# Two fused cross-attention layers on one core: the first layer's row maxima, turned kind by head and brought in by two transfers of four heads

## The chip, the cores and the metric

The kernel runs on one core of one Trainium2 chip. The metric is the device time of one execution in microseconds (us). Three executions before the change took 1526.58, 1529.79 and 1536.33 us, with a median of 1529.79 us. One more execution was recorded by the hardware profiler, and all profile lines come from it.

Engines are named as the profile names them. PE is TensorE (matmuls; PEld are its weight loads), DVE is VectorE, ACT is ScalarE, POOL is GpSimd, and SP is SyncE, which here only issues transfers. Rows marked ACTq or SPq are transfers (DMAs) issued by ACT or SP.

## The reference

Two attention layers follow each other on `x` (16 batches, 256 positions, 320 channels, 20 heads of 16). Both read the same context of 256 tokens. What matters here is the first layer, which splits the context in 77 text tokens and 179 image tokens and takes a softmax over each of the two kinds apart:

```python
q, k_text, v_text = hidden_states @ Wq, text @ Wk, text @ Wv
probs = softmax(einsum('bhqd,bhkd->bhqk', q_h, k_h) * scale)
text_out = einsum('bhqk,bhkd->bhqd', probs, v_h)
scores = einsum('bhqd,bhkd->bhqk', q_h, ip_k_h) * scale
text_probs = softmax(einsum('bqc,bkc->bqk', q, k_text) * scale)
q_sem = einsum('bqk,bkc->bqc', text_probs, text)
sem = einsum('bqc,bnc->bqn', q_sem, ip) * scale
ip_probs = softmax(scores + 0.5 * sem[:, None]) * spatial_mask[None, None, :, None]
ip_out = einsum('bhqk,bhkd->bhqd', ip_probs, ip_v_h)
out = (text_out + ip_out) @ Wout + bout + residual
```

So each query row of each head needs two maxima in this layer: one over its 77 text scores and one over its 179 image scores. The second layer is of the same family, with 252 text tokens, 4 image tokens and one maximum for a row.

## The kernel before

The code counts the layers from 0, so the first layer of the reference has names that end in 0, and its 80 units of work are k = 0 to 79. A unit is four heads of one batch (five units a batch). The second layer has another 80 units, k = 80 to 159, and names that end in 1. One loop runs over all units (`slot0`, then `slot1`), and next to each unit the steps of other tasks (keys, queries, the semantic map, the output projection, weights) are called at times that tables in the code give.

**A unit of the first layer.** Its operands lie in two stacks, `qs` and `ks`, of 128 partitions by four heads by 256. There are four buffers of each, used in turn. Partitions 0 to 47 hold the 16 numbers of a head in three parts (rounded part and remainder), 48 to 124 hold the text map (`tph` on the side of `qs`, `M` on the side of `ks`), and partitions 125 and 126 (`XROW + T0` and the next) hold in `ks` two rows of minus ones, one for text tokens and one for image tokens, and in `qs` the two row maxima of each head. So a product over all 127 rows gives scores from which the maxima are already taken away. The steps are:

1. `stacks0(k)`, four units ahead: SP loads `ks` and `qs` (the DMAs from `kd`, `qd`, `tph`, `M`).
2. `score0(k, t)` for each half t of the queries: four matmuls (line 738) fill the only score tile `S` of this layer, and two DVE reductions (lines 739 and 740) write the maxima over text and over image tokens to `mn`.
3. `maxima0(k)`: two small matmuls by the identity (line 746) turn `mn` into 8 rows of 256 in a bank X of PSUM, ACT copies them to the SBUF tile `mt` (line 748), and four transfers issued by ACT (line 750) bring two rows each, a head's text and image maximum, to partitions 125 and 126 of that head in `qs`. For units 0 and 1 SP issues them. `mt` has one buffer, so the next copy waits for these transfers.
4. `turned0(k, t)`, a slot later: four matmuls (line 762) into two T tiles, two exponentials on ACT (line 765) to `P`, two products on POOL (line 768).
5. `attend0(k)`: 24 matmuls (line 795), then DVE and POOL work (`settle0`).

In slot k the code gives PE this order: maxima of unit k+1, scores of unit k+2 (t = 0), turned scores of unit k (t = 0), other tasks, attend of unit k-1, scores of unit k+2 (t = 1), turned scores of unit k (t = 1), loads of unit k+4, other tasks. The second exponentials of unit k are tied behind the last maxima transfer of unit k+1 (`queued(exp, issues[k + 1])`).

**Other tasks that the prediction names.** `semantic0` adds two score parts: ACT copies one from its bank X (`sp`, line 663), DVE adds the other (line 664) and so frees the bank, then come a maximum (667), the exponential (ACT, 672) and the division (ACT, 676). `context` casts loaded tokens (`rawc`) on ACT to `cta` and `ctb` (line 160). `split` casts the attended rows `hT` on ACT to `ho` (lines 592 and 593) for the output projection (lines 605 and 608). `evacuate` takes keys and queries out of a bank X (lines 160, 267 to 270). There are three X banks, used in turn by all tasks.

**What sets the order.** PE's order is that in which the code calls. In the loop over units the orders of DVE, ACT, POOL and SP are made by the framework's scheduler when the program is built, with its own estimates of durations; `queued` and `anchor` tie a few instructions. In the built program the transfers of SP and ACT share eight semaphores, which they take in turn. A transfer may be issued only when the transfer that had its semaphore before, eight earlier in the program, has landed; where another wait implies this, the wait is left out. A waiting transfer holds everything behind it on its engine.

Of the kernel before, what the change touches and what calls it, by code (L numbers as in the profile page):

```python
# [9 lines left out]
FR = mybir.dt.float32r  # L10
AF = mybir.ActivationFunctionType
ALU = mybir.AluOpType
AX = mybir.AxisListType
# [10 lines left out]
T0 = 77  # L24
# [7 lines left out]
KS0 = 127  # L32
KS1 = 50
XROW = 48
# [15 lines left out]
def xattn2(  # L50
# [27 lines left out]
    nc = tc.nc  # L78
    f = lambda ap: ap.bitcast(F32)
    mm = nc.tensor.matmul  # L80
# [9 lines left out]
    def bank(tag="X"):  # L90
        return ps.tile([128, 512], F32, tag=tag, name=tag, bufs=BANKS[tag])
# [10 lines left out]
    def scores(kept=False):  # L102

        s = whole if kept else ps.tile([128, 1024], F32, tag="S", name="S", bufs=1)
        return s.rearrange("p (h t) -> p h t", h=4)
# [4 lines left out]
    def buf(tag, shape, dtype=F32, bufs=1, name=None):  # L110
        if tag in ("wB", "wD", "vr", "raw"):
            return sb.tile(shape, dtype, tag=tag, name=name or tag, bufs=bufs)
        size = 1
        for d in shape[1:]:
            size *= d
        if tag not in slots:
            slots[tag] = [0, dtype] + [const_tile([128, max(size, words.get(tag, 0))], f"{tag}_{i}", dtype) for i in range(bufs)]
        n, kind, *ring = slots[tag]
        assert kind == dtype and len(ring) == bufs, tag
        slots[tag][0] += 1  # L120
        t = ring[n % bufs][: shape[0], :size]
        names = "abcd"[: len(shape) - 1]
        if len(names) > 1:
            t = t.rearrange(f"p ({' '.join(names)}) -> p {' '.join(names)}", **dict(zip(names, shape[1:])))
        return t

    def const_tile(shape, tag, dtype=F32):
        return const.tile(shape, dtype, tag=tag, name=tag)
# [7 lines left out]
    ident_r = const_tile([128, 128], "ident_r", FR)  # L136
# [15 lines left out]
    def anchor(inst):  # L152
        anchors[inst.ins.engine] = inst
        return inst
# [574 lines left out]
    maxes, issues = {}, {}  # L729

    def score0(k, t):
        Q, K = QK[k]
        if t == 0:
            maxes[k] = buf("mn", [128, 2, 4, 2], FR, bufs=2)
        mn = maxes[k]
        sp = scores(True)
        for h in range(4):
            mm(sp[:, h], Q[: XROW + T0, h, t * 128 : (t + 1) * 128], K[: XROW + T0, h], start=True, stop=True)  # L738
        nc.vector.tensor_reduce(mn[:, t, :, 0], sp[:, :, :T0], axis=AX.X, op=ALU.max)  # L739
        anchor(nc.vector.tensor_reduce(mn[:, t, :, 1], sp[:, :, T0:], axis=AX.X, op=ALU.max))  # L740

    def maxima0(k, queue=nc.scalar):
        Q, mn = QK[k][0], maxes[k]
        mp = bank()
        for t in range(2):
            mm(mp[:8, t * 128 : (t + 1) * 128], mn[:, t].rearrange("p h a -> p (h a)"), ident_r, start=True, stop=True)
        mt = buf("mt", [8, S], FR)
        nc.scalar.copy(mt, mp[:8, :S])  # L748
        for h in range(4):
            issues[k] = queue.dma_start(f(Q[XROW + T0 : KS0, h]), f(mt[2 * h : 2 * h + 2]))  # L750

    def turned0(k, t):

# [386 lines left out]
    for c in range(B // 2):  # L1140
        n, k = 10 * c, [("k0", c)] if c else []
# [34 lines left out]
    def ahead(k, t):  # L1176
        if k < NS:
            score0(k, t)
        else:
            both1(k - 2, t)  # L1180
# [5 lines left out]
    def begin():  # L1186
# [15 lines left out]
        stacks0(2)  # L1202
        parts(k0)
        score0(0, 0)
        parts(v1)
        score0(0, 1)
        get("m0t", 1)
        maxima0(0, nc.sync)
        parts(v1)
        get(*v1)  # L1210
# [3 lines left out]
        score0(1, 1)  # L1214
        parts(*[("s0", 1)] * 3)
        maxima0(1, nc.sync)
        parts(("s0", 1), ("s0", 1), ("k0", 1))
        resid0.append(load(xT_d[0], "xc"))
# [97 lines left out]
```

## Time and profile before

| what | value |
|---|---|
| median of three runs | 1529.79 us |
| profiled execution, whole time | 1526.5 us |
| its span, first to last instruction | 1524.7 us |
| PE busy in the span | 1436.7 us (94%) |
| POOL busy | 1209.5 us (79%) |
| DVE busy | 1114.5 us (73%) |
| ACT busy, its DMA issues not counted | 891.4 us (58%) |

In the profiled execution the first units' work starts at about 50 us, the first layer's loop runs from about 70 to 706 us, and the second layer to the end. A group's row names line, engine, operation and tiles. A row of waits says which instruction waited for which, then the total, the number of times and the longest (us). In a timeline the brackets at a row's end give the idle time of the engine before it and what ended it. The clock column (PEclk) is the granted TensorE clock as a share of full speed.

### The profile page before, as it was taken

What the parts mean: (1) busy time and instruction counts of PE and PEld (TensorE: products, weight loads), DVE (VectorE), ACT (ScalarE), POOL (GpSimd) and SP (SyncE); (2) the same over time, 40 slices, a digit from 0 to 9 for tenths busy, and PEclk for the clock granted to TensorE, in tenths of its full rate; (3) what the DMA queues carried; (4) which work ended last, traced back from release to release, by engine and by line L of the source; (5) the groups of instructions that cost most, each with busy time, mean ns of one, the idle gap of its engine ahead of it and who ended that gap; (6) DMA issues with size and microseconds to landing.
All of it is one profiled execution on the core that took longest, in us unless ns stands there. A gap on an engine that the chain in (4) does not pass through costs nothing.

```text
span 1524.7 us, 36323 instructions
## 1 busy us (share of the span) xinstructions
PE 1436.7 (94%) x12726; PEld 1159.4 (76%) x12726; DVE 1114.5 (73%) x2543; ACT 891.4 (58%) x2037; POOL 1209.5 (79%) x1529
## 2 busy tenths in 40 slices
PE   6789999999999989879999999999999999999996
PEld 6678888888888868667777777777777777777764
DVE  5466767676767677876787877787777777787784
ACT  5346565656565645546666666666666666666561
POOL 4269898989888976789678787878787787878695
PEclk9899999999999999999999999999999999999998
DMA  6766766676767675776354344444444444533411
GB/s 210 206 189 180 214 190 212 187 219 188 218 185 221 187 205 138 215 200 180 98 146 127 106 129 129 120 121 135 112 116 135 119 118 121 144 106 105 111 33 37
DMA packets 228818, 233.07 MB, mean 153 GB/s; under 512 B 38410, under 2 KB 198508, under 8 KB 228620
## 3 DMA queue, kind: packets, MB, share of 16 engines
q1 hardware_dynamic: 226428, 229.44, 52.6%
q8 instruction: 102, 1.67, 0.5%
q10 hardware_dynamic: 2208, 1.30, 0.3%
q14 instruction: 80, 0.66, 0.1%
HBM read 118.04 MB, written 77.10 MB: 128 GB/s over the span
## 4 chain that ended last, share of the span: by engine, by line
PE 75%; DVE 6%; DMA 6%; POOL 6%; ACT 2%; issue 2%; SPq 1%; ACTq 1%; POOLq 0%; DVEq 0%
PE X L935 16%; PE X L248 14%; PE X L605 6%; PE P L795 6%; PE P L947 5%; PE S L738 5%; PE P L957 4%; PE T L887 3%; PE S L893 3%; PE T L762 3%; DMA rawc<-in_cT_dram 2%; POOL P L768 2%; PE X L608 2%; PE X L564 2%; PE X L258 2%
## 5 line engine op out<-in xcount | busy, mean ns | idle before, releaser
L768 POOL TENSOR_TENSOR P<-P,rs 128x512 f32<-128x512 f32 x320 | 408.7, 1303 | 94.9 <-ACT P L765 93.4
L926 POOL TENSOR_TENSOR wt<-P,ctb 128x512 f32<-128x512 f32 x320 | 405.9, 1290 | 81.6 <-ACT ctb L925 81.6
L935 PE MATMUL X<-ctb,gm 128*128 128x512 f32 x1120 | 308.0, 402 | 0.5 <-DVE hT L1070 0.2
L765 ACT ACTIVATE P<-T 128x512 f32<-128x512 f32 x320 | 175.6, 594 | 156.4 <-PE T L762 116.9
L936 DVE TENSOR_TENSOR wt<-X,wt 128x512 f32<-128x512 f32 x320 | 216.2, 680 | 45.9 <-PE X L935 43.3
L935 PEld LDWEIGHTS X<-ctb,gm 128*128 128x128 f32 x1120 | 194.5, 189 | 36.3 <-PE X L935 5.3
L907 ACT ACTIVATE P<-T 128x512 f32<-128x512 f32 x320 | 172.9, 593 | 63.7 <-PE T L887 60.2
L925 ACT ACTIVATE ctb<-P 128x512 fp32r<-128x512 f32 x320 | 186.1, 626 | 23.7 <-PE X L935 20.4
L895 DVE TENSOR_REDUCE mn<-S 128x4 fp32r<-128x1008 f32 x160 | 191.4, 1196 | 0.0
L740 DVE TENSOR_REDUCE mn<-S 128x4 fp32r<-128x716 f32 x160 | 142.5, 890 | 0.0
L795 PE MATMUL P<-P,vr 128*32 128x256 f32 x1920 | 126.9, 394 | 1.8 <-DVE tmp L812 1.5
L738 PE MATMUL S<-ks,qs 125*128 125x256 f32 x640 | 118.3, 308 | 6.2 <-DMA qs<-tph 3.9
L738 PEld LDWEIGHTS S<-ks,qs 125*128 125x128 f32 x640 | 89.0, 195 | 41.5 <-issue 25.4
L762 PE MATMUL T<-qs,ks 127*128 127x256 f32 x640 | 108.7, 292 | 5.7 <-ACT P L765 5.0
L739 DVE TENSOR_REDUCE mn<-S 128x4 fp32r<-128x308 f32 x160 | 74.4, 465 | 32.6 <-PE S L738 31.2
L762 PEld LDWEIGHTS T<-qs,ks 127*128 127x128 f32 x640 | 91.4, 196 | 8.9 <-ACT P L765 7.3
L806 DVE STREAM_TRANSPOSE nt<-P 128x512 f32<-128x512 f32 x80 | 57.0, 712 | 46.8 <-PE P L795 46.0
L795 PEld LDWEIGHTS P<-P,vr 128*32 128x32 f32 x1920 | 56.2, 112 | 43.7 <-issue 7.2
L947 PE MATMUL P<-P,v1t 128*32 128x256 f32 x1280 | 86.4, 388 | 0.0
L605 PE MATMUL X<-ho,wF 128*128 128x256 f32 x512 | 76.0, 291 | 8.8 <-ACT mt L748 5.3
L957 PE MATMUL P<-wt,zone 128*32 128x256 f32 x1280 | 84.2, 379 | 0.0
L605 PE MATMUL X<-hq,wE 128*128 128x256 f32 x512 | 75.7, 291 | 6.6 <-ACT hq L592 4.0
(237 smaller groups left out, 2979.9 us busy)
## 6 DMA issues: line engine op xcount, KB each, us to landing
qd<-q SPq DMA_DIRECT2D x96, 256.0 KB
qs<-tph SPq DMA_DIRECT2D x64, 308.0 KB
rawc<-in_cT_dram SPq DMA_DIRECT2D x60, 256.0 KB
qs<-qd SPq DMA_DIRECT2D x80, 192.0 KB
ks<-kd SPq DMA_DIRECT2D x80, 192.0 KB
ks<-kd SPq DMA_DIRECT2D x160, 96.0 KB
qs<-qd SPq DMA_DIRECT2D x160, 96.0 KB
kd<-kst SPq DMA_DIRECT2D x57, 256.0 KB
```

Source lines behind the costliest of these rows:

```text
L248: last = mm(out, lhs(a, k), rhs(b, k), start=i == 0, stop=i == len(terms) - 1)
L605: mm(pp, w(s, k, m), a[:, t], start=i == 0, stop=i == len(terms) - 1)
L738: mm(sp[:, h], Q[: XROW + T0, h, t * 128 : (t + 1) * 128], K[: XROW + T0, h], start=True, stop=True)
L762: mm(st[p][:, j], K[:KS0, 2 * p + j, t * 128 : (t + 1) * 128], Q[:KS0, 2 * p + j], start=True, stop=True)
L765: exp = anchor(nc.scalar.activation(pt, st[p], AF.Exp, scale=SCALE))
L768: anchor(nc.gpsimd.tensor_mul(pt, pt, rs[:, t : t + 1].to_broadcast([128, 2, S])))
L795: mm(pv[32 * s : 32 * s + 32, o : o + S], v[:, vt, h : h + 32], P[k, s // 2][:, t, s % 2], start=vt < 2, stop=vt != 1,)
L895: anchor(nc.vector.tensor_reduce(maxes[k + 2][:, t], sp[:, :, :T1], axis=AX.X, op=ALU.max))
L925: nc.scalar.activation(R[k, u][:, t], P[k, u][:, t], AF.Copy, scale=0.5)
L926: anchor(nc.gpsimd.tensor_sub(W[k, u][:, t], P[k, u][:, t], f(R[k, u][:, t])))
L935: mm(yp, gm[:, gb], R[k, u][:, kt], start=i == 0, stop=i == len(blocks[n]) - 1)
L936: nc.vector.tensor_mul(W[k, u][:, n], yp, W[k, u][:, n])
```

## The change

The maxima tile `mn` is laid out by kind and then head, not by head and then kind: `mn[:, t, 0]` holds the four text maxima and `mn[:, t, 1]` the four image maxima. The turned 8 rows in `mt` are then the four heads' text maxima and after them the four heads' image maxima. Two transfers bring them in: each takes four partitions of `mt` (1 KB each) and writes one partition of `qs`, over its four heads (4 KB). The sizes of the reductions, the matmuls and the copy stay as they are. One line is added, so later lines have numbers higher by one.

```diff
@@ -731,23 +731,24 @@
     def score0(k, t):
         Q, K = QK[k]
         if t == 0:
-            maxes[k] = buf("mn", [128, 2, 4, 2], FR, bufs=2)
+            maxes[k] = buf("mn", [128, 2, 2, 4], FR, bufs=2)
         mn = maxes[k]
         sp = scores(True)
         for h in range(4):
             mm(sp[:, h], Q[: XROW + T0, h, t * 128 : (t + 1) * 128], K[: XROW + T0, h], start=True, stop=True)
-        nc.vector.tensor_reduce(mn[:, t, :, 0], sp[:, :, :T0], axis=AX.X, op=ALU.max)
-        anchor(nc.vector.tensor_reduce(mn[:, t, :, 1], sp[:, :, T0:], axis=AX.X, op=ALU.max))
+        nc.vector.tensor_reduce(mn[:, t, 0], sp[:, :, :T0], axis=AX.X, op=ALU.max)
+        anchor(nc.vector.tensor_reduce(mn[:, t, 1], sp[:, :, T0:], axis=AX.X, op=ALU.max))
 
     def maxima0(k, queue=nc.scalar):
         Q, mn = QK[k][0], maxes[k]
         mp = bank()
         for t in range(2):
-            mm(mp[:8, t * 128 : (t + 1) * 128], mn[:, t].rearrange("p h a -> p (h a)"), ident_r, start=True, stop=True)
+            mm(mp[:8, t * 128 : (t + 1) * 128], mn[:, t].rearrange("p a h -> p (a h)"), ident_r, start=True, stop=True)
         mt = buf("mt", [8, S], FR)
         nc.scalar.copy(mt, mp[:8, :S])
-        for h in range(4):
-            issues[k] = queue.dma_start(f(Q[XROW + T0 : KS0, h]), f(mt[2 * h : 2 * h + 2]))
+        for a in range(2):
+            row = XROW + T0 + a
+            issues[k] = queue.dma_start(f(Q[row : row + 1]), f(mt[4 * a : 4 * a + 4]))
 
     def turned0(k, t):
 
```

Over the whole program the transfers of `mt` into the first layer's stacks go from 320 to 160 (ACT issues 312 of them before and 156 now). PE's instructions stand in the same order as before. The scheduler puts instructions of ACT, DVE, POOL and SP in other places; three of these places on ACT follow. Names: `mt` are the turned maxima, `P` the exponentials, `ctb` casts of context, `sp` the semantic scores, `kst` keys, `q` queries, `ho` the attended rows, numbers are buffers. In each list time runs down.

The first place is where the second half of a pair of batches' context is cast. Before, on ACT:

```order
L160 CAST ctb_85<-rawc_94 128x512
L748 CAST mt_213<-X 8x256
L750 DMA qs_206<-mt_213 2x256
L160 CAST ctb_86<-rawc_93 128x512
L765 ACTIVATE P_96<-T 128x512
L765 ACTIVATE P_97<-T 128x512
L750 DMA qs_206<-mt_213 2x256
```

Now, on ACT:

```order
L748 CAST mt_213<-X 8x256
L160 CAST ctb_85<-rawc_94 128x512
L751 DMA qs_206<-mt_213 1x4x256
L766 ACTIVATE P_96<-T 128x512
L766 ACTIVATE P_97<-T 128x512
L751 DMA qs_206<-mt_213 1x4x256
L160 CAST ctb_86<-rawc_93 128x512
```

The cast of `ctb_86` stood ahead of the unit's first pair of exponentials and stands behind it now; the cast of `ctb_85` and the copy of `mt` changed places.

The second place is a unit later, where the semantic scores' softmax runs. Before, on ACT:

```order
L663 COPY sp_377<-X 128x77
L672 ACTIVATE sp_376,mx_380<-sp_376,mx_380 128x77
L160 CAST kst_254<-X 128x2x77
L748 CAST mt_213<-X 8x256
L765 ACTIVATE P_98<-T 128x512
L765 ACTIVATE P_99<-T 128x512
L750 DMA qs_203<-mt_213 2x256
L676 ACTIVATE sp_376<-sp_376,mx_380 128x77
L750 DMA qs_203<-mt_213 2x256
L672 ACTIVATE sp_377,mx_381<-sp_377,mx_381 128x77
L750 DMA qs_203<-mt_213 2x256
L676 ACTIVATE sp_377<-sp_377,mx_381 128x77
```

Now, on ACT:

```order
L663 COPY sp_377<-X 128x77
L672 ACTIVATE sp_376,mx_380<-sp_376,mx_380 128x77
L676 ACTIVATE sp_376<-sp_376,mx_380 128x77
L672 ACTIVATE sp_377,mx_381<-sp_377,mx_381 128x77
L676 ACTIVATE sp_377<-sp_377,mx_381 128x77
L160 CAST kst_254<-X 128x2x77
L748 CAST mt_213<-X 8x256
L751 DMA qs_203<-mt_213 1x4x256
L766 ACTIVATE P_98<-T 128x512
L766 ACTIVATE P_99<-T 128x512
L751 DMA qs_203<-mt_213 1x4x256
L160 CAST kst_254<-X 128x2x179
```

The first pair of exponentials (`P_98`, `P_99` at line 765, now 766) stood right behind the copy of `mt` and ahead of all transfers. It now stands behind both steps of the second `sp` half, the copy of `mt` and one transfer. The steps of `sp` stood between the transfers and now stand ahead of them.

The third place is two units later, ahead of the output projection. Before, on ACT:

```order
L691 ACTIVATE rs_504<-X 128x512
L750 DMA qs_205<-mt_213 2x256 x3
L765 ACTIVATE P_98<-T 128x512
L765 ACTIVATE P_99<-T 128x512
L267 CAST kst_254<-X 64x2x179
L268 COPY both_301<-X 64x358
L593 ACTIVATE ho_256<-hT_1311,tmask 128x256
L267 CAST q_248<-X 64x256
L268 COPY both_300<-X 64x256
L748 CAST mt_213<-X 8x256
L765 ACTIVATE P_96<-T 128x512
```

Now, on ACT:

```order
L691 ACTIVATE rs_504<-X 128x512
L751 DMA qs_205<-mt_213 1x4x256
L593 ACTIVATE ho_256<-hT_1297,tmask 128x256
L766 ACTIVATE P_98<-T 128x512
L766 ACTIVATE P_99<-T 128x512
L267 CAST kst_254<-X 64x2x179
L268 COPY both_301<-X 64x358
L267 CAST q_248<-X 64x256
L268 COPY both_300<-X 64x256
L748 CAST mt_213<-X 8x256
L766 ACTIVATE P_96<-T 128x512
```

The cast of `ho` (line 593) stood among the copies that lead to `mt` and now stands ahead of the second pair of exponentials of the unit before.

Counted over the built programs: before, 156 of ACT's 312 transfers carry a wait for a semaphore's earlier transfer, now 98 of 156. Such a waiting transfer stands ahead of a unit's first exponential in 6 units before and in 35 now, and ahead of its second pair in 73 units before and in 66 now.

## The prediction

> **What bounds the kernel now.** I read the busy times by stage first.
>
> ```profile
> core 0: us, PE busy (x) PEld busy (x) DVE busy (x) ACT busy (x) POOL busy (x), PEclk, DMA share, GB/s
> 0.00:70.00 70.00, 49.87 (x280) 46.27 (x281) 34.03 (x108) 31.79 (x81) 21.47 (x32) 0.92 0.71 210
> 70.00:160.00 90.00, 80.31 (x718) 67.76 (x718) 60.05 (x135) 47.48 (x116) 69.58 (x67) 0.97 0.66 192
> 160.00:520.00 360.00, 346.55 (x3252) 298.16 (x3251) 248.89 (x603) 209.37 (x502) 319.28 (x309) 1.00 0.70 200
> 520.00:706.00 186.00, 159.54 (x1411) 130.82 (x1410) 143.52 (x319) 94.41 (x228) 150.36 (x150) 0.94 0.67 188
> 706.00:1490.00 784.00, 779.09 (x6946) 600.75 (x6946) 611.64 (x1343) 502.90 (x1102) 630.25 (x926) 1.00 0.42 118
> ```
>
> PE binds. In the second layer (706 to 1490 us) it is idle for 5 of 784 us, and the change leaves that layer's work alone. In the first layer PE is idle for 9.7, 13.4 and 26.5 us in the stages from 70 us on, 49.6 together. No more than that, and what a lower clock costs, can be gained there. POOL is next, with 319 of 360 us. So the question is which of PE's waits hang on ACT's transfers. PE's own waits, in the steady stage (160 to 520 us) and then in the next:
>
> ```profile
> PE X L605 <- ACT mt L748: 4.4, 5, 0.9
> PE X L248 <- DVE sp L664: 4.2, 4, 1.1
> PE T L762 <- ACT P L765: 2.6, 3, 1.0
> PE X L746 <- DVE mn L740: 1.3, 5, 0.3
> PE X L608 <- ACT mt L748: 0.7, 2, 0.4
> ...
> PE X L680 <- ACT sp L676: 4.0, 1, 4.0
> PE T L762 <- ACT P L765: 2.4, 2, 1.7
> ```
>
> The steady stage's 13.2 us come nearly all from ACT, directly or through the `sp` that DVE adds after ACT's copy. What ACT itself waits for in the same stage:
>
> ```profile
> ACT P L765 <- PE T L762: 65.5, 52, 3.1
> ...
> ACT ctb L160 <- DMA rawc<-in_cT_dram: 13.9, 7, 3.4
> ...
> ACT P L765 <- DMA qs<-mt: 11.1, 4, 3.5
> ACT sp L676 <- DMA ks<-M: 6.5, 4, 2.0
> ```
>
> ACT mostly waits for PE (65.5 us). So it isn't the bound on average; it is late only at a few places in each period of ten units, and there PE pays. The last two rows are instructions held behind a maxima transfer that itself waits for an older transfer.
>
> **What goes: issue time.** The maxima's rows:
>
> ```profile
> L750 ACTq DMA_DIRECT2D qs<-mt x312: 569/570/1205, 74.8 to 708.4; - x156
> L917 ACTq DMA_DIRECT2D qs<-mt x160: 632/632/707, 712.2 to 1483.8; - x160
> ...
> L750 SPq DMA_DIRECT2D qs<-mt x8: 562/588/690, 54.8 to 64.6; - x8
> ```
>
> A transfer of two rows of 1 KB holds ACT for 0.57 us, the second layer's of 4 KB for 0.63 us. The new form (4 KB, four heads) is not in the trace; I take 0.63, the row of the same size, with 0.57 and twice that, 1.14, as ends. ACT's issuing goes from 312 x 0.57 = 178 us to 156 x 0.63 = 98 us: 80 us less, or 1.0 us for each of 78 units (0 at the upper end). Very little of it is on PE's path, since ACT waits for PE anyway. I therefore price PE's waits one by one, by what stands ahead of them on ACT now.
>
> ```profile
> 374.62 0.62 ACT L160 CAST ctb<-rawc 128x512 fp32r<-128x512 f32 x1 [3.43 <-DMA rawc<-in_cT_dram]
> ...
> 375.14 0.59 ACT L765 ACTIVATE P<-T 128x512 f32<-128x512 f32 x1
> ...
> 375.79 0.99 PE L762 MATMUL T<-qs,ks 127*128 127x256 f32 x4 [0.95 <-ACT P L765]
> ...
> 376.11 0.23 ACT L663 COPY sp<-X 128x77 f32<-128x77 f32 x1
> ...
> 376.37 0.24 DVE L664 TENSOR_TENSOR sp<-sp,X 128x77 f32<-128x77 f32 x1 [2.96 <-ACT sp L663]
> ...
> 381.56 1.25 PE L248 MATMUL X<-cta,wB 128*128 128x360 f32 x6 [1.05 <-DVE sp L664]
> ```
>
> First place of the change: the cast of `ctb_86` held ACT for 3.43 us, and the exponentials behind it made PE wait 0.95 us; the same delay ran through `sp` and DVE to PE's wait of 1.05 us, six microseconds later. Now the exponentials stand ahead of that cast. The steady stage has 2.6 us of the first kind, which I take off whole: **-2.6**. Of the second kind it has 4.2 us. The copy of `sp` (663) still stands behind the cast, but DVE now adds the second `sp` half ahead of two reductions, so I take all: **-4.2** (0 at the other end). What is late next is DVE's reduction of `S`, moved behind those steps (below).
>
> ```profile
> 403.34 0.51 ACT L593 ACTIVATE ho<-hT,tmask 128x256 fp32r<-128x256 f32 x1
> ...
> 404.65 0.36 ACT L748 CAST mt<-X 8x256 fp32r<-8x256 f32 x1
> ...
> 405.07 1.20 PE L605 MATMUL X<-ho,wF 128*128 128x256 f32 x8 [0.89 <-ACT mt L748]
> ```
>
> Third place: PE waits 0.89 us for the bank that the copy of `mt` frees. The cast of `ho` ahead of it, 0.51 us, now runs earlier, where ACT had been waiting for PE. Five times 0.5: **-2.5** (of 5.1 with line 608; 0 if `hT` comes too late).
>
> The same waits stand before and after the steady stage. The first of these rows is that of 70 to 160 us, and the same row stands again at 520 to 610 us, where the other two are from:
>
> ```profile
> PE X L248 <- DVE sp L664: 1.0, 1, 1.0
> ...
> PE X L605 <- ACT mt L748: 0.9, 1, 0.9
> PE T L762 <- ACT P L765: 0.7, 1, 0.7
> ```
>
> By the same working 1.0 + 1.0 + 0.5 + 0.7: **-3.2**. At the front SP issues four transfers less, 4 x 0.59 = 2.4 us, ahead of loads that PE later waits for; half of it counts: **-1.2** (0 to -2.4). The wait of 4.0 us at line 680 stands behind one such transfer and two loads of weights; those stay, and I take **-0.9** for the transfer's part.
>
> **What comes: the first transfer ahead of the exponentials.** In the second place ACT used to run a unit's first exponentials right behind the copy of `mt`. Now both `sp` steps and a transfer stand ahead. The transfer may wait for the one that had its semaphore before, and behind it wait the exponentials; for these waits PE (the T tiles) and then POOL. What such a wait costs is in the trace once, plainly:
>
> ```profile
> 682.58 1.08 ACT L765 ACTIVATE P<-T 128x512 f32<-128x512 f32 x2 [3.28 <-DMA qs<-qd]
> ...
> 683.23 1.29 PE L762 MATMUL T<-qs,ks 127*128 127x256 f32 x4 [1.67 <-ACT P L765]
> ```
>
> ACT was held 3.28 us and PE lost 1.67. I expect less in the second place, because the copy of `mt` itself comes later there and the older transfers have landed by then: 0.6 us of PE in each of six periods, **+3.6** (0 to 10, which is six times 1.67). DVE's reductions moved behind the `sp` steps lie inside this figure. POOL and SP keep the same work. The landing of the new form is not in the trace; the last transfer is now issued earlier in most units, and PE's waits for landing were small:
>
> ```profile
> PE T L762 <- DMA qs<-mt: 0.5, 2, 0.3
> ...
> PE T L887 <- DMA qs<-mt: 3.4, 3, 1.6
> ...
> q10 hardware_dynamic: 2208, 1.30, 0.3%
> ```
>
> so landing counts 0. As its end I take the second row, that of the second layer's 4 KB form: +3.4. [...]
>
> **The sum.** -2.6 - 4.2 - 2.5 - 3.2 - 1.2 - 0.9 + 3.6 = **-11.0 us**. The profiled execution took 1526.5 us, 1.8 more than its span of 1524.7 and 3.3 less than the median of the runs, 1529.79. The differences are stated against the median: 1529.8 - 11 = **1518.8, so 1519 us**. The ends of the terms give -18 (no added wait, and line 605, line 608 and the front in full) to +7 (the second kind, line 593 and the front at 0, the added wait 10 and the landing 3.4).
>
> **The rivals.**
> - *Hidden anyway.* PE takes the same time because each removed wait reappears at the next buffer: the X banks, the one `S` tile or POOL at 319 of 360 us. For it speaks that ACT waits for PE 65.5 us; against, that PE's steady waits name ACT and not POOL. Time: 1526 to 1533, about 1529.
> - *More than forecast.* From 520 to 706 us PE's granted clock is 0.94 and in the steady stage 1.00. If the waits behind transfers shrink here too, the clock recovers with them. Bound: 0.06 x 186 = 11 us on top of the sum: 1508. For it speaks that the clock is low just where the waits are long; against, that most of these waits are for loads of weights, which stay. [...]
> - *Slower: the transfer holds the first exponentials.* In 35 units, against 6, a transfer with a semaphore wait stands ahead of the first exponential. If the older transfer is still in flight in each of the 29 new ones, PE loses about 1 us a time (2.6 us in 3 waits is 0.9; 1.67 once): +29, less the 11 gained: 1530 + 18 = 1548. It decides once the older transfer lands over some 2 us after the copy of `mt`, since ACT held 3.28 cost PE 1.67. Against it: with fewer transfers, eight back lies further back in time.
> - *The change does not do what it says*: the new transfer takes twice the issue time (1.14 us). Then ACT's issuing stays at 178 us, the order is still the new one, and the time is that of the first rival.
>
> **How the numbers follow.** Forecast (1512 to 1526): 0.55. Hidden or issue not saved (1526 to 1533): 0.22. More (1505 to 1512): 0.12. Slower (1535 to 1550): 0.11. The range from 1508 to 1534 leaves out the last case and half of the third, under 0.2. A measurement of this kernel tells about 1% from no change, 15 us. Faster by over 1%, under 1514.5: all of "more" and a fifth of the forecast, 0.24. Slower by over 1%, over 1545: the worse part of the slower case, 0.07. Within 1%: 0.69.
>
> **What would show it.** In the profile after: 156 ACT transfers of `mt` near 0.6 us, with an issue time of 1.1 refuting the first step; the row of line 605 waiting for `mt` down from 4.4 to about 2; the `sp` row (4.2) near zero; PE busy in the steady stage above 97%. The wait of T for `P` (2.6) should move to the second place, at about 0.6 us a period; if it reaches 10 us or more, the slower rival is right. If PE's idle time from 70 to 706 us stays near 49.6 us with other names on it, the first rival is. The prediction is wrong as well if the second layer's stage changes at all.

## The result, and the profile after

The changed kernel takes 1522.74 us (median of 16 runs, 1515.87 to 1530.51). The kernel before, run beside it, takes 1530.09 us (16 runs, 1522.94 to 1537.66). The ratio is 0.995, with a 95% interval of 0.9928 to 0.9972: about 7.4 us or 0.5% faster, inside the 1% that I counted as no change. The profiled execution took 1519.03 us, with a span of 1517.2 us (before: 1526.5 and 1524.7).

The busy time by stage of the changed kernel, in the same stretches as shown of before:

```profile
core 0: us, PE busy (x) PEld busy (x) DVE busy (x) ACT busy (x) POOL busy (x), PEclk, DMA share, GB/s
0.00:70.00 70.00, 48.80 (x273) 44.86 (x274) 33.73 (x108) 32.20 (x82) 21.64 (x31) 0.92 0.71 214
70.00:160.00 90.00, 83.88 (x730) 71.84 (x729) 60.17 (x138) 48.01 (x116) 70.14 (x69) 0.93 0.66 191
160.00:520.00 360.00, 349.89 (x3302) 302.55 (x3301) 252.04 (x609) 213.36 (x506) 324.21 (x314) 0.99 0.70 203
520.00:706.00 186.00, 162.32 (x1458) 131.32 (x1457) 142.99 (x331) 98.51 (x238) 152.94 (x154) 0.94 0.68 191
706.00:1490.00 784.00, 777.55 (x6903) 599.19 (x6902) 608.31 (x1334) 499.32 (x1092) 627.79 (x925) 1.00 0.41 116
```

In the steady stage PE is busy for 3.3 us more than before (349.89 against 346.55), and 3.6 and 2.8 us more in the stage ahead of it and the one behind. The waits of PE in the steady stage, all that are over half a microsecond:

```profile
PE X L248 <- POOL ctb L163: 4.0, 4, 1.0
PE X L605 <- ACT mt L748: 2.8, 5, 0.9
PE X L746 <- DVE mn L740: 2.7, 4, 0.9
PE S L738 <- DMA qs<-qd: 0.6, 1, 0.6
```

The wait of T for the exponentials (2.6 us) is gone, and so is that of X for `sp` (4.2 us). But a wait for POOL's `ctb`, which was not there, has come at nearly the size of the second one. It is at another product of the same line 248. Two or so microseconds of line 605's 5.1 (with line 608) are gone. The waits of ACT in that stage (its exponentials now have line number 766, one higher than before, and T has 763):

```profile
ACT P L766 <- PE T L763: 66.5, 63, 2.7
...
ACT ctb L160 <- DMA rawc<-in_cT_dram: 12.0, 8, 2.6
...
ACT P L766 <- DMA qs<-mt: 3.8, 2, 2.7
```

The instructions that issue the maxima's transfers, and the packets of ACT's queue:

```profile
L751 ACTq DMA_DIRECT2D qs<-mt x156: 580/581/1218, 72.5 to 696.3; - x156
...
L751 SPq DMA_DIRECT2D qs<-mt x4: 612/640/712, 55.4 to 63.6; - x4
```

```profile
q10 hardware_dynamic: 2208, 1.30, 0.3%
```

A transfer of four heads is issued in 0.58 us, as fast as one of two rows (0.57), and the queue carries the same number of packets. What takes the place of the old waits, in the timeline behind unit 39's copy of `mt`:

```profile
372.00 0.62 ACT L160 CAST ctb<-rawc 128x512 fp32r<-128x512 f32 x1 [1.82 <-DMA rawc<-in_cT_dram]
...
373.55 1.29 POOL L163 TENSOR_TENSOR ctb<-rawc,ctb 128x512 fp32r<-128x512 f32 x1
...
374.89 0.45 PE L248 MATMUL X<-ctb,wA 128*128 128x156 f32 x2 [0.98 <-POOL ctb L163]
```

The load lands late as before; the exponentials no longer stand behind its cast, but the product that needs `ctb` itself now waits for cast and subtraction.

**How far the clock makes the time.** Within the runs of one kernel the time follows the mean granted clock: over 29 runs of the kernel before, span and clock have a correlation of -0.89, at clocks from 0.970 to 0.982, and on the line through them 0.001 of clock goes with 1.4 us. I therefore give, beside each time, the mean over the runs of span times granted clock, as an aid to tell less waiting from more clock. It is 1484.5 us (standard error 0.7) for the changed kernel and, in the groups of runs of the kernel before, 1492.9 to 1494.9 us. By this measure the change takes 8 to 10 us of work and waiting off; the clock itself hardly differs (0.976, against 0.976 to 0.978 in the groups of the kernel before).

### The profile page after: what moved, and what is told of

Read it like the earlier page. It is cut to its first block, busy times and chain, and to the rows that moved or that the text cites. A ratio compares the mean times of both kernels' runs of the same rounds, so it can differ in the third digit from the quotient of the medians.

```text
span 1517.2 us, 36085 instructions
## 1 busy us (share of the span) xinstructions
PE 1436.4 (95%) x12726; PEld 1160.3 (76%) x12726; DVE 1107.7 (73%) x2543; ACT 894.1 (59%) x2037; POOL 1209.4 (80%) x1529
## 2 busy tenths in 40 slices
DMA packets 228815, 233.04 MB, mean 154 GB/s; under 512 B 38410, under 2 KB 198508, under 8 KB 228620
## 3 DMA queue, kind: packets, MB, share of 16 engines
q10 hardware_dynamic: 2208, 1.30, 0.3%
## 4 chain that ended last, share of the span: by engine, by line
PE 73%; POOL 8%; DMA 6%; DVE 6%; ACT 3%; issue 2%; SPq 2%; ACTq 0%; POOLq 0%; DVEq 0%
PE X L936 15%; PE X L248 13%; PE X L605 6%; PE P L796 6%; PE S L738 5%; PE P L948 5%; PE P L958 4%; PE T L763 4%; PE T L888 3%; PE S L894 3%; POOL P L769 2%; POOL wt L927 2%; PE X L608 2%; PE X L258 2%; PE X L564 2%
```

## The experiments

All times are medians, and each ratio is against runs of the kernel before on the same chip. Each edit is made in the changed kernel, whose two lines of the loop over transfers are written as one, so that the line numbers are those of before.

| kernel | transfers per unit, and queue | us | ratio (95%) | span x clock, us | PE busy of 360 us |
|---|---|---|---|---|---|
| before | 4, ACT | 1530 to 1531 | 1 | 1492.9 to 1494.9 | 346.55 |
| kind4 | 4, ACT | 1532.88 | 1.001 (0.9985 to 1.0035) | 1494.7 | 346.43 |
| after2 | 2, ACT | 1522.72 | 0.9934 (0.991 to 0.9959) | 1486.2 | 349.74 |
| pin | 2, ACT, old first place | 1526.76 | 0.9966 (0.9944 to 0.9987) | 1487.5 | 347.14 |
| early | 2, ACT, four load buffers | 1525.27 | 0.996 (0.9942 to 0.9977) | 1488.9 | 348.10 |
| dve | 2, ACT, subtraction on DVE | 1532.28 | 1.0019 (0.9998 to 1.0039) | 1491.6 | 342.38 |
| dummy | 2, ACT, landing not waited for | 1521.98 | 0.994 (0.9921 to 0.996) | 1484.2 | 348.20 |
| one | 1, ACT | 1525.70 | 0.996 (0.9935 to 0.9985) | 1489.1 | 349.89 |
| kind8 | 8, ACT | 1769.91 | 1.1573 (1.153 to 1.1616) | 1617.6 | 289.78 |
| none2 | 0 | 1512.87 | 0.9873 (0.9845 to 0.9902) | 1478.3 | 354.27 |
| sp2 | 2, SP | 1519.61 | 0.9934 (0.991 to 0.9959) | 1485.2 | 352.10 |
| onesp | 1, SP | 1517.22 | 0.9906 (0.9885 to 0.9928) | 1485.6 | 354.89 |
| onesp2 | 1, SP, once more | 1513.34 | 0.9897 (0.9869 to 0.9926) | 1484.6 | 352.18 |

### The layout alone (kind4)

```diff
-        for a in range(2):
-            issues[k] = queue.dma_start(f(Q[XROW + T0 + a : XROW + T0 + a + 1]), f(mt[4 * a : 4 * a + 4]))
+        for a, h in ((0, 0), (0, 2), (1, 0), (1, 2)):
+            issues[k] = queue.dma_start(f(Q[XROW + T0 + a : XROW + T0 + a + 1, h : h + 2]), f(mt[4 * a + h : 4 * a + h + 2]))
```

> The changed layout of the maxima (kind by head), but brought in by four transfers of two heads of one row each, as many as before; the order of every engine's instructions is then that of the kernel before. Theory A (the gain comes from the number of transfers: ACT's issue time, the waits behind transfers and the order that follows from them): the gain is gone, 1530 us, ratio to the kernel before 0.998 to 1.002. Theory B (the gain comes from the layout itself: turned rows that land earlier, reductions into runs of four): as fast as the changed kernel, 1523 us, ratio 0.995.

The time is that of the kernel before, ratio 1.001. The sequence of PE's and of DVE's instructions is exactly the old one; on ACT and on POOL one step of `ho`, near 695 us, stands a place earlier. The waits of PE in the steady stage of kind4 are of the old kinds:

```profile
PE X L605 <- ACT mt L748: 4.4, 5, 0.9
PE X L248 <- DVE sp L664: 3.8, 4, 1.1
PE X L608 <- ACT mt L748: 3.2, 3, 2.0
PE T L762 <- ACT P L765: 1.5, 1, 1.5
```

So the layout is worth nothing by itself: the whole gain comes from the number of transfers and from the order that goes with it.

### The same kernel again (after2)

> The changed kernel once more (two lines of its loop written as one, nothing else), for a second profile and a second comparison. Ratio 0.993 to 0.997. If the 2.8 us that the second layer gave back in the first pair of profiles were an effect of the change, the stage from unit 80 on takes again some 2 to 3 us longer than in the kernel before; if it was noise, the difference lies elsewhere or has another sign. The drop of the granted clock to 0.5 at 376 to 378 us shows again if it is tied to the wait of 0.98 us for the subtraction of ctb on POOL.

Ratio 0.9934 against 0.995 in the first comparison. PE is busy for 349.74 us of the steady stage, and the wait for POOL's `ctb` is 3.9 us in four. What differs between the profiles is told by the start of the n-th copy of `mt` (lines 748 and, from unit 80 on, the second layer's), minus that in the profile of before; the last column is that of the span:

| profile | unit 0 | unit 12 | unit 59 | unit 79 | span |
|---|---|---|---|---|---|
| changed kernel | +0.3 | -0.9 | -5.6 | -10.3 | -7.5 |
| after2 | +1.8 | +0.2 | -3.5 | -5.9 | -2.6 |
| kind4 (layout alone) | +0.2 | -2.2 | +1.3 | +0.9 | +6.6 |

After unit 80 all three lose 3 to 6 us against the profile of before, kind4 most, although it has the old number of transfers and the old order. So the second layer's part need not be an effect of the change; it seems that the one profile of before was a good one there. Section "What the runs showed of the hardware" below shows one such loss.

### The old order at the first place (pin)

The cast of `ctb_86` is remembered, and the next two exponentials are queued behind it:

```diff
...
+                if pin and i == len(parts):
+                    pins.append(casts[0])
...
+            if pins:
+                queued(exp, pins[0])
+                pins[:] = pins[p:]
```

> The changed kernel with one thing of the old order put back: the cast of ctb_86 stands ahead of the unit's exponentials again (two transfers per unit as in the change). Theory A (at the first place the new order exchanges one wait for another): in the stage from 160 to 520 us the waits of T for P (2 to 3 us) and of X for sp (3 to 4 us) come back and the wait of X for POOL's ctb (4.0 us) goes; the time rises by 2 to 4 us over the changed kernel, 1525 to 1527 us. Rival (the gain of the first place is nothing: the wait for ctb was as dear as the two that it replaced): 1522 to 1523 us, the same idle time of PE in that stage. Rival C (the new order of the first place is harmful, since the wait for ctb is followed by a lower granted clock): 1518 to 1521 us.

1526.76 us, ratio 0.9966: the loss of 2 to 4 us that theory A gives. The clock has a part in it; span times clock rises by 1.3 to 3 us. PE's waits in the steady stage (T's line is 766 here, the exponentials' 769):

```profile
PE T L766 <- ACT P L769: 8.7, 4, 2.5
PE X L609 <- ACT mt L752: 4.0, 5, 0.9
```

The wait for `ctb` is gone and that of T for the exponentials is back, but at 8.7 us in four, more than the 2.6 that before had. The casts of `ctb` wait longer for their loads, 17.2 us in seven times against 13.9 before; where the one quoted in the prediction waited 3.43 us, now

```profile
375.55 0.62 ACT L160 CAST ctb<-rawc 128x512 fp32r<-128x512 f32 x1 [4.46 <-DMA rawc<-in_cT_dram]
```

The two transfers ahead of it are both issued by 372.1 us, so they don't hold it. The wait for `sp` did not come back. So the new order at this place is worth some microseconds, but less than the 2.6 + 4.2 = 6.8 at which I priced its two rows; the wait for `ctb` is its cost, paid once in a period. Pin isn't the old place in full either, since its loads come later.

### Taking away the new wait (early, dve)

Early gives the context's four loads of a period four buffers, and the code asks for all four at the start, so that those of `ctb` needn't wait for the casts of `cta`:

```diff
-"rawc raw" if b == 2 and n == 2 else "rawc"
+"rawc raw" if n == 2 else "rawc"
```

> The changed kernel with the context's four loads of a period in four buffers (rawc, rawc, raw, raw) and not in two used twice, so that the loads of ctb don't wait for the casts of cta. Theory A (the new wait of PE for POOL's ctb, 4.0 us in the steady stage, comes from the late load: the cast of ctb waits 11 to 12 us in all for rawc): that wait goes, PE busy from 160 to 520 us rises from 349.9 to about 353, and the time falls by 3 to 5 us to about 1518 us. Rival (the next wait takes its place, mt's copy or mn's reduction): PE's busy time in that stage stays within 1 us, 1522 us.

The wait for `ctb` is gone, and the time isn't better: 1525.27 us. PE's first wait in the steady stage of this kernel:

```profile
PE S L738 <- DMA qs<-qd: 5.9, 3, 2.1
```

S waits for the stack of Q. I take it that the loads of `ctb`, issued earlier, now stand ahead of that stack's load in SP's queue; the runs don't show this by itself. The rival is right in that another wait takes the place.

The time is lost later, though. By the copies of `mt`, this kernel needs 7.7 us less than the kernel before from unit 12 to unit 59, where the changed kernel needs 4.7 and after2 3.7 less; from unit 59 to unit 79 it needs 6.9 us more. PE is busy for 153.24 of the 186 us from 520 to 706 us (162.32 in the changed kernel), and its longest wait there is

```profile
PE X L661 <- DVE xc L843: 7.5, 2, 6.8
```

So the idea seems to work in the steady stage and to be undone behind it. Why DVE is late with `xc` there is open, and this is one profile.

Dve moves the subtractions of context tiles in the first layer from POOL to DVE (and those of one batch in the second layer from DVE to POOL):

```diff
-nc.gpsimd if wait and b != 2 else nc.vector)
+nc.vector if n == 2 else nc.gpsimd)
```

> The changed kernel with the subtraction of each context tile's rounded half (cta, ctb) on DVE and not on POOL. It takes away the wait of PE for POOL's ctb (four times 1.0 us in the steady stage) if that is POOL's lateness. Theory A: that wait halves or goes, 1518 to 1521 us. Rival (the wait hangs on ACT's cast, which waits for the load): the same 4 us under DVE's name and 20 subtractions more on DVE ahead of its reductions, 1522 to 1526 us.

1532.28 us: past the figures of theory A and of the rival, and all of the gain is lost. PE's first waits in the steady stage of this kernel are those for DVE's reductions of the one `S` tile and for its subtraction of `q`:

```profile
PE S L738 <- DVE mn L740: 8.8, 4, 2.2
PE X L661 <- DVE q L270: 6.3, 4, 1.8
```

The wait for `ctb` is gone from the list here too. What POOL did for PE at a price of 4.0 us, DVE does at 15.1, with other work of its own behind it.

### No transfers (none2)

```diff
-        for a in range(2):
+        for a in range(2 if k < 2 * SIZES["NR"] else 0):
...
-AF.Exp, scale=SCALE))
+AF.Exp, scale=1e-4 * SCALE))
```

> The changed kernel with the maxima transfers left out for all units but the first eight; the exponentials of the first layer take a scale 10,000 times smaller so that they stay finite (left out: the shift by the row maxima and the right scale; same instructions and shapes). It bounds what the transfers still cost. Theory A (each transfer costs issue time on ACT's way to PE's waits): 3 to 6 us less than the changed kernel, 1517 to 1520 us. Rival (what is left isn't the transfers'): 1522 to 1524 us.

Left out are the transfers and with them the shift by the row maxima, so the results are not those of the other kernels. A first form (none), without the smaller scale, gave no time: some of its exponentials were not finite.

1512.87 us, ratio 0.9873: 9 to 10 us under the changed kernel, more than I expected. The steady stage of none2:

```profile
160.00:520.00 360.00, 354.27 (x3381) 306.73 (x3381) 259.23 (x626) 217.39 (x522) 332.48 (x323) 1.00 0.73 208
```

So from four transfers to two the kernel gains some 8 us and from two to none 9 to 10. In this kernel the cast of `ctb` stands ahead of the exponentials again, and it costs nothing, because it comes sooner: 1.8 us after the start of the copy of `mt` at unit 39 (366.87 and 365.03 us), where in after2 it comes 4.7 us after it (372.37 and 367.65). There is no wait for `ctb` and none of T for the exponentials in the steady stage.

### Landing or issue (dummy)

```diff
-queue.dma_start(f(Q[XROW + T0 + a : XROW + T0 + a + 1]), f(mt[4 * a : 4 * a + 4]))
+queue.dma_start(f(Q[XROW + T0 + a : XROW + T0 + a + 1] if k < 2 * SIZES["NR"] else QK[k][a][127:]), f(mt[4 * a : 4 * a + 4]))
```

(with the exponentials' scale of none2; the results differ here too, since the maxima arrive in a row that nothing reads)

> The changed kernel with its two transfers per unit issued as they are, in the same order on every engine, but from the ninth unit on into row 127 of the Q and K stacks, which nothing reads: PE's T no longer waits for their landing (left out: the shift by the row maxima; the exponentials of the first layer take a scale 10,000 times smaller so that they stay finite). With the kernel without transfers (1513 us) and the changed kernel (1522 us) it splits the 9 us that two transfers still cost. Theory A (ACT's issue time, the waits for a semaphore ahead of an issue and the order around them): 1520 to 1523 us, no faster than the changed kernel. Rival (the landing, for which T waits): 1513 to 1516 us.

1521.98 us, ratio 0.994; the changed kernel's ratios are 0.995 and 0.9934. Not to wait for the landing saves nothing. The waits of PE that lead the steady stage are the changed kernel's too:

```profile
PE X L248 <- POOL ctb L163: 4.0, 4, 1.0
PE X L605 <- ACT mt L748: 2.8, 5, 0.9
PE X L746 <- DVE mn L740: 1.7, 3, 0.8
```

So the 9 to 10 us lie with what is issued, and these runs don't divide them: ACT's time for it, the semaphores that it waits for, and the order that it leaves for the rest.

### One transfer on ACT, and eight (one, kind8)

```diff
-        for a in range(2):
-            issues[k] = queue.dma_start(f(Q[XROW + T0 + a : XROW + T0 + a + 1]), f(mt[4 * a : 4 * a + 4]))
+        for a in range(1):
+            issues[k] = queue.dma_start(f(Q[XROW + T0 : KS0]), f(mt))
```

> The changed layout with a single transfer of both kinds, eight rows of 1 KB, per unit. Theory A (the number of transfers decides): 78 issues of about 0.6 us less on ACT than in the changed kernel; by the share that the first halving brought on PE's path (7 us of 80 saved) another 3 to 5 us, 1518 to 1520 us. Rival (the waits left now name POOL, DVE and loads, not transfers): no further gain, 1522 to 1525 us. Rival C (the single transfer lands later, since it has to carry eight rows at once): T waits for landing, some 0.5 us in each of 78 units at most, so up to 1550 us.

1525.70 us: no better than two, by its first rival. In the steady stage it is the same as two, with the same leading wait:

```profile
160.00:520.00 360.00, 349.89 (x3315) 302.91 (x3315) 254.16 (x613) 213.47 (x509) 326.25 (x317) 1.00 0.71 204
```

```profile
PE X L248 <- POOL ctb L163: 4.1, 4, 1.1
```

Fewer transfers alone don't move that wait, as long as `ctb`'s cast stands where it does and its load lands when it does. The 3 us by which the median is worse than two lie outside this stage. From 520 to 706 us PE is busy for 155.82 us, against 160.05 in after2 and 162.32 in the changed kernel; which wait makes them I have not settled.

Kind8 brings every row by its own transfer, eight per unit.

```diff
+        for a, h in [(a, h) for a in range(2) for h in range(4)]:
+            issues[k] = queue.dma_start(f(Q[XROW + T0 + a : XROW + T0 + a + 1, h]), f(mt[4 * a + h : 4 * a + h + 1]))
```

> The changed layout with eight transfers of one row each per unit, four more than the kernel before. Theory A (a price per transfer: from four to two 8 us, from two to none 9 us, so 4 to 4.5 us for each transfer of a unit): 1531 + 4 x 4.3 = 1548 us, 1540 to 1560. Rival (only the order that two transfers happened to get counts): within 5 us of the kernel before, 1526 to 1536 us.

1769.91 us, ratio 1.157, far outside both expectations. The price per transfer is no constant. PE's first wait over the whole span of this kernel, its transfers on ACT, and the packets of ACT's queue:

```profile
PE T L762 <- DMA qs<-mt: 143.7, 86, 4.9
```

```profile
L750 ACTq DMA_DIRECT2D qs<-mt x624: 503/600/1925, 71.5 to 948.5; - x156
```

```profile
q10 hardware_dynamic: 20928, 1.34, 0.8%
```

Eight issues of 0.6 us are 4.8 us for a unit, and the exponentials of other units lie between them; T needs the last transfer of all, and waits 143.7 us. Here the landing is on PE's path, which it isn't with two (T waits 1.0 us for it in the changed kernel's first layer). Of the 240 us lost, span times clock accounts for 123; the rest is clock, whose mean falls to 0.914. The form of the transfers changes here with their number (each row goes in 32 packets, last section), and this run doesn't tell the two apart.

### The transfers on SP (sp2, onesp, onesp2)

```diff
-    def maxima0(k, queue=nc.scalar):
+    def maxima0(k, queue=nc.sync):
```

> The changed kernel with the first layer's two maxima transfers issued by SP and not by ACT: ACT loses all 156 issues (about 90 us), the landing stays, and SP's queue gets them behind its loads. Theory A (ACT's issue time is what counted): 1518 to 1521 us, if SP is not late. Rival (SP's queue waits for buffers ahead of a transfer, so the transfer is issued late and T waits for its landing): more than 1530 us, with rows of T waiting for the transfer of some us.

1519.61 us, ratio 0.9934, the same as after2. In the steady stage PE is busier (352.10 of 360 us) and its wait for `ctb` is gone; in the next stage SP is late with a load and with a stack:

```profile
PE X L746 <- DMA rawc<-in_wvi_dram: 2.3, 1, 2.3
...
PE T L762 <- DMA qs<-mt: 1.7, 2, 1.4
```

With one transfer (the edit of one) SP has half of that to issue.

> One transfer of eight rows per unit, issued by SP and not by ACT. By the price per transfer (none: 1513 us; two on SP: 1520 us) about 1516 us, ratio 0.990. Rival (a single transfer lands later, as the one on ACT, 1525.7 us, or SP is late with it): 1520 to 1526 us.

> One transfer of eight rows per unit on SP's queue once more, for a firm comparison with the changed kernel (ratios 0.9934 to 0.995 in three comparisons). If it beats the changed kernel: ratio 0.988 to 0.992 again, and PE busy from 160 to 520 us again near 355 of 360 us at a granted clock of 1.00. If the first comparison was luck of the clock: 0.993 to 0.995.

1517.22 and 1513.34 us, ratios 0.9906 and 0.9897. This beats both kernels: 1.0% under the kernel before and 0.3 to 0.5% under the changed one, whose three comparisons (the first, after2 and, with the same order, dummy) gave 0.9934 to 0.995. The steady stage of the first of the two:

```profile
160.00:520.00 360.00, 354.89 (x3379) 306.40 (x3377) 258.43 (x626) 217.20 (x521) 332.01 (x321) 1.00 0.74 209
```

That is as much as without any transfer (354.27); in onesp2 it is 352.18, short of the 355 expected. So in the steady stage PE waits 5 and 2 us less than in the changed kernel. Over the whole program, span times clock is no lower (1485.6 and 1484.6 against 1484.5 and 1486.2), and the mean granted clock is 0.9805 and 0.9817 against 0.976 and 0.978. By that measure the gain over the changed kernel is in the clock; how far shorter waits make the higher clock, the runs don't show.

## Why the prediction was right, and where it was wrong

Predicted were 1519 us, 11 us of gain; measured are 1522.74 and 7.4. The range from 1508 to 1534 holds it, and the likeliest case (within 1%) is what came. By its steps:

- **Issue time (0.63 us taken).** 0.58 us was measured, hardly dearer than the old form's 0.57, so the rival that the change doesn't do what it says is out. That only part of the 80 us of issue time would count was right: 7 to 8 us came of it.
- **T's wait for the exponentials, -2.6.** Right: the row is gone in both profiles of the changed kernel.
- **X's wait for `sp`, -4.2.** This is the step that failed. The row went, but 4.0 us of wait for POOL's `ctb`, which the sum doesn't have, came at another product of line 248, so of the term's 4.2 us about 0.2 are left. The prediction looked for what is late next and named DVE's reduction of `S`; it never followed the cast that it had moved back to its own reader. That cast, the subtraction behind it and the product that needs both were in the code. The row of the 3.43 us wait for `rawc` said that the load was late, whatever stood behind the cast. This is the first rival's mechanism ("each removed wait reappears"), right at this one place, and with POOL, against which I had argued. As a whole that rival doesn't hold: PE's idle time from 70 to 706 us, which by it would stay near 49.6 us, falls to 39.9, and to 42.7 in after2.
- **Line 605, -2.5.** Right in size: 5.1 us with line 608 became 2.8.
- **The second place, +3.6.** Wrong on the safe side: no wait of T for the exponentials is left in the steady stage. ACT's own waits behind a transfer there are 3.8 us in the one profile and 10.9 in after2, and PE's T waits for none of them. What rose is PE's wait for DVE's `mn`, from 1.3 to 2.7 us (1.7 in after2), which I had put inside this term. The slower rival, built on the same mechanism, falls with it.
- **Outside the steady stage, -3.2, and line 680, -0.9.** The part ahead, priced at 1.0, brought 1.2 and 1.6 us (units 0 to 12) in the two profiles, and the part behind, priced at 2.2, brought 4.8 and 2.5 (units 59 to 79), so the places are right. Line 680 is not a part of it: its wait rose from 4.0 to 4.9 us.

```profile
PE X L680 <- ACT sp L676: 4.9, 1, 4.9
```

- **The front, -1.2.** Not seen: the copy of unit 0 comes 0.3 and 1.8 us later than in the profile of before.
- **Landing, 0.** Shown by dummy, whose ratio without the wait for the landing is 0.994, against 0.995 and 0.9934 with it. In the changed kernel T's wait for the transfer is 1.0 us over the whole first layer, where it was 0.5, and in one, whose single transfer brings all eight rows, it is 0.5 us in the steady stage. How many packets such a transfer has is shown by the row of ACT's queue in onesp, where it carries the second layer's transfers alone, and then in one:

```profile
q10 hardware_dynamic: 960, 0.66, 0.2%
```

```profile
q10 hardware_dynamic: 1740, 1.30, 0.3%
```

The difference of 780 is ten packets for each of 78 transfers.
- **The second layer unchanged.** It takes 3 to 6 us longer than in the profile of before, most of all in kind4, which has the old transfers' number and order, so by itself this is no sign against the step.
- **More than forecast, by the clock.** Not in the changed kernel (0.94 from 520 to 706 us as before, and 0.99 in the steady stage). It came with the single transfer on SP, where the mean clock was higher by about half a per cent.

The steady stage alone was priced at -2.6 - 4.2 - 2.5 + 3.6 = -5.7 us. Measured are -2.6 - 0.2 - 2.3 + 1.4 + 0.6 (the new wait of S for `qd`) = -3.1, which is the 3.3 us that PE is busier. The sum was 4.0 us too hopeful with `ctb` and 2.2 too careful with the second place (3.6 against the 1.4 of `mn`), so the two errors cancel by half; that is luck. What is left in this stage, 2.6 us, is most of the 3.6 by which forecast and result differ. The remaining 1 us can't be given to any term: 0.001 of the mean granted clock goes with 1.4 us in the 29 runs above.

## What to carry to other kernels

When a reordering takes an instruction out of the way of others, follow the instruction itself to its own reader: here the cast that waits for a late load moved its wait along with it, 4.0 us at `ctb` against the 4.2 that went, and the price of the old place was not the gain. Price transfers on a compute engine's queue by the order they force as much as by their issue time; where the layout allows, let one transfer on a queue with room do the work of four (here ratios of 0.9906 and 0.9897 with one on SP, against 0.9934 to 0.995 with two on ACT). And before a gain of half a per cent is explained from a pair of profiles, take the granted clock out (span times clock; 0.001 of clock went with 1.4 us here), and take a second profile of the same program.

## What the runs showed of the hardware

One short wait of PE can be followed by a stretch at half clock. The wait of 0.98 us for `ctb` at 374.89 us in the changed kernel, in stretches of 2 us (the column before the last two is the granted clock):

```profile
374.00:376.00 2.00, 1.11 (x8) 0.88 (x9) 1.97 (x7) 1.76 (x6) 2.00 (x2) 0.99 0.86 274
376.00:378.00 2.00, 2.00 (x11) 2.00 (x10) 0.84 (x6) 1.38 (x6) 2.00 (x3) 0.50 0.78 216
378.00:380.00 2.00, 2.00 (x10) 1.94 (x8) 1.51 (x3) 1.26 (x3) 2.00 (x4) 0.65 0.93 257
380.00:382.00 2.00, 2.00 (x29) 1.07 (x28) 0.78 (x2) 0.50 (x2) 2.00 (x3) 1.00 1.03 312
```

The clock is short by 0.50 x 2 + 0.35 x 2 = 1.7 us there, more than the wait itself. In kind4 the same follows a wait of S for `mn` in the second layer, 1.4 us; the same matmul doesn't wait in the profile of before, with the same order of PE. First kind4's wait, then its stretches:

```profile
PE S L893 <- DVE mn L895: 1.4, 1, 1.4
```

```profile
774.00:776.00 2.00, 0.70 (x7) 0.59 (x7) 1.93 (x5) 1.06 (x2) 1.12 (x2) 0.92 0.99 281
776.00:778.00 2.00, 2.00 (x8) 1.62 (x7) 1.76 (x4) 0.36 (x1) 0.11 (x1) 0.50 0.53 185
778.00:780.00 2.00, 2.00 (x12) 1.86 (x12) 0.69 (x1) 0.48 (x2) 0.30 (x2) 0.72 0.01 2
```

Waits of the same size aren't always followed by it. Those of 0.95 and 1.05 us at 375.79 and 381.56 us, quoted in the prediction, were not; the profile of before around them:

```profile
374.00:376.00 2.00, 1.05 (x9) 0.75 (x6) 0.00 (x0) 1.38 (x3) 0.87 (x2) 1.00 0.92 261
376.00:378.00 2.00, 2.00 (x17) 1.81 (x17) 1.60 (x6) 1.95 (x6) 2.00 (x3) 1.00 0.43 130
...
380.00:382.00 2.00, 0.95 (x8) 0.75 (x7) 1.90 (x7) 1.45 (x3) 2.00 (x3) 1.00 0.86 237
382.00:384.00 2.00, 2.00 (x19) 1.68 (x22) 0.28 (x2) 0.45 (x2) 2.00 (x4) 1.00 0.89 242
```

Nor is it bound to a place of the program. In after2 the wait for `ctb` at 375.16 us (0.99 us) has a granted clock of 1.00 behind it, and the one a period earlier, at 298.26 us (0.97 us), does not:

```profile
298.00:300.00 2.00, 1.54 (x8) 1.24 (x9) 1.97 (x9) 1.41 (x5) 2.00 (x3) 0.74 0.86 270
300.00:302.00 2.00, 2.00 (x10) 2.00 (x10) 0.84 (x5) 1.60 (x6) 2.00 (x3) 0.50 0.83 203
```

So by these rows I estimate the cost of a wait of 1 us at between 1 and 2.7 us (1.0 and the 1.7 above), and two profiles of one program differ by such stretches at different places (376 to 380 us in the changed kernel, 298 to 302 us in after2). With the correlation of span and clock above (-0.89), I take them for the larger part of this kernel's spread of half a per cent; no run shows that by itself. Nor do the runs show why the clock falls behind one such wait and not behind another.

The other surprise is the form of a transfer of one row. Kind8's 20928 packets, less the 960 of the second layer's transfers, are 32 for each of 624 transfers of 1 KB; in the changed kernel four rows of 1 KB make eight, (2208 - 960) / 156. So a single row went in 32 packets here, and the packets under 512 B rose from 38410 in the changed kernel to 58250. The issue time of these 624 transfers, 0.60 us, is near that of the larger ones (0.57 us for two rows, 0.58 for four).
